# Layer 1's causal attention: 32 steps of one query block each, or 16 steps of blocks i and 7-i together

## The chip, the cores and the metric

The kernel runs on one core of a Trainium2 chip. A core has a matrix engine (TensorE, PE in the profile, with its weight loads as PEld), a vector engine (VectorE, DVE), an activation engine (ScalarE, ACT), a general engine (GpSimd, POOL) and SyncE (SP), which issues most transfers. Each works through its own instructions in order, and they wait for each other by semaphores. SBUF is the working memory of 128 partitions; PSUM takes TensorE's results, in 8 banks of 512 float32 numbers for each partition. The metric is the device time of one execution in microseconds (us), as the median of several runs.

## The reference, cut to what matters

Two transformer layers on x of shape (2, 1024, 256). Each layer adds an attention and a feed-forward of the same normalized input. The change concerns the attention of the second layer, which has 16 heads, queries of 128 + 64 numbers and keys and values that all heads share (64 numbers of latent and 64 rotated ones):

```python
q = rmsnorm(hidden_states @ wq_a.T, q_a_ln_w) @ wq_b.T          # 16 heads x (128 + 64)
ckv = hidden_states @ wkv_a.T                                    # 64 + 64, one for all heads
kv = rmsnorm(ckv[..., :64], kv_a_ln_w)
q_pe, k_pe = apply_rope(q_pe, cos, sin), apply_rope(k_pe, cos, sin)
q_abs = jnp.einsum('bhsd,hdc->bhsc', q_nope, q_absorb)
scores = (einsum('bhsc,btc->bhst', q_abs, kv) + einsum('bhsd,bxtd->bhst', q_pe, k_pe)) * SCALE
attn = softmax(where(causal, scores, finfo.min))                 # 1024 x 1024, lower triangle
x = jnp.einsum('bhst,btc->bhsc', attn, kv)
x = jnp.einsum('bhsc,hdc->bhsd', x, out_absorb)                  # then @ wo.T
```

A query block is 128 tokens, and there are 8 for each of the 2 batches. Block i needs keys 0 to 128(i+1) only, so block 0 has 128 keys and block 7 has 1024.

## The kernel before, in words

The first 764 us compute layer 0, the feed-forward of layer 1 and the projections that its attention needs; weights are folded there, so that a query of two heads comes out of three small matmuls (`wpe`, `folded["wm"]`, `folded["w2"]`) and the output needs one product with `folded["wvo"]`. The keys lie in `kT`, the values four times over the partitions in `vrep`. The attention follows as one order written out by hand (`tc.manual_schedule()`): each engine runs its instructions in the order in which the code names them, while the loads on SP are placed by the scheduler where they fit.

A step is a batch b, a query block i and a half g of the 16 heads, so 32 steps. Batch 0 goes from block 0 up to block 7, batch 1 from block 7 down to block 0. At any time three steps overlap: `s` computes scores, `prev` (the step before) is multiplied with the values, and `older` (two before) is normalized and projected to the output.

- `scores(s, h)`: TensorE multiplies a head's query with the keys into a PSUM pair (2 banks, L1055). VectorE adds the mask, writes the result to `p` and reduces the row's maximum, all in one instruction (L1060). ScalarE takes the exponential and its sum (L1063). A block with more than 512 keys takes a whole pair for a head; with 512 or fewer, two heads share a pair, one bank each.
- `turn_over` (L1068): VectorE transposes the weights in 32 x 32 squares into `pT`.
- `product(s, sb)` (L1094): eight small matmuls side by side in the array for each block of 32 values, into `ps_o`, which takes 4 banks.
- `inverse`, `inverse_T`, `normalize`: 1/sum is spread by GpSimd (L1075), transposed by TensorE (L1083), copied by ScalarE (L1087), and multiplied with `ps_o` by VectorE (L1103).
- `output` and `add` (L1115, L1125): the projection, and the addition to the row of x that was fetched from memory.
- `query_half`: the query of a coming step: `project` (L988, L994) on TensorE into a pair, `latent` (L1027) on ScalarE, `rotate` (L1009 to L1020) on VectorE, ScalarE and GpSimd. `t1` and `t2` are single buffers.

PSUM holds two pairs under the tag "s", which scores, queries, transposes and outputs take in turn, and the one `ps_o`: all 8 banks. For blocks 4 to 7 a step has four cycles of two heads, for blocks 0 to 3 two cycles of four heads. Each cycle first names its scores, then in cycle 0 the normalization and the next query, in cycle 1 the output, in the last the transposes, then a share of the products, then the turn-overs. A step has 4(i+1) value blocks, dealt over one to four cycles by a rule of its size.

## The time and the profile before

| | us |
|---|---|
| median of 3 runs (1473.28 to 1475.24) | 1473.69 |
| the profiled execution's own time | 1469.04 |
| its span, first to last instruction | 1467.3 |
| TensorE busy | 1327.6 |
| VectorE busy | 790.8 |
| ScalarE busy | 671.2 |
| GpSimd busy | 443.8 |
| first score of layer 1's attention | 770.00 |

The span is what the profile's lines add up to; the run's own time has a little more around it. A row of the profile names the line of the code, the engine, the operation, the tile written and those read, the shape, the count, the busy time and the mean of one, and the idle time ahead of it with what ended that. TensorE's times are modelled at their ends, so a busy TensorE need not be at its peak; the granted clock says how much of its full speed it had.

### The profile page before, as it was taken

Reading aid. Unit: us, or ns where it says so; the run is one execution under the profiler, and the core shown is the slowest. Engines: PE = TensorE matmul, PEld = TensorE weight load, DVE = VectorE, ACT = ScalarE, POOL = GpSimd, SP = SyncE. Lnnn points to the kernel's source line nnn. Section 1 sums busy time; section 2 is a strip of 40 time slices with the busy share of each in tenths; the row PEclk is TensorE's granted clock in tenths of the full one; section 3 lists DMA queues with packets and bytes.
Section 4 is the critical chain, followed back from the end, with each engine's and each line's share of the span. In section 5 each row is a group of like instructions: output and inputs, shape, how many; then the busy total and the mean of one; then the engine's idle time right before and its main releaser. Section 6 shows DMA issues by size and latency. Waiting matters only on the chain.

```text
span 1467.3 us, 36387 instructions
## 1 busy us (share of the span) xinstructions
PE 1327.6 (90%) x15614; PEld 795.9 (54%) x15614; DVE 790.8 (54%) x1939; ACT 671.2 (46%) x1234; POOL 443.8 (30%) x480
## 2 busy tenths in 40 slices
PE   5689999898999989999996777999999999998886
PEld 2233445354563533465775554666666676665565
DVE  3765545454456553134333455666777767665543
ACT  2234563453638546643314444545454454444442
POOL 2223433333414211003304332434233233423330
PEclk9659999899999999999996999999999999999988
DMA  5121301010100000001233000000000000000000
GB/s 202 55 34 57 99 8 23 0 23 1 23 5 18 23 1 18 15 1 54 73 88 49 12 10 4 13 13 13 13 3 14 13 3 14 13 14 13 9 9 16
DMA packets 56977, 39.27 MB, mean 27 GB/s; under 512 B 37200, under 2 KB 52816, under 8 KB 56560
## 3 DMA queue, kind: packets, MB, share of 16 engines
q1 hardware_dynamic: 55968, 33.67, 8.5%
q8 instruction: 122, 2.00, 0.6%
q0 software_dynamic: 416, 2.49, 0.4%
q10 hardware_dynamic: 432, 0.79, 0.2%
q14 instruction: 39, 0.32, 0.1%
HBM read 24.35 MB, written 10.49 MB: 24 GB/s over the span
## 4 chain that ended last, share of the span: by engine, by line
PE 85%; DVE 7%; ACT 3%; issue 2%; POOL 2%; DMA 1%; SPq 0%; DVEq 0%; ACTq 0%; POOLq 0%
PE ps_s L1055 19%; PE ps_m L307 11%; PE ps_o L1094 10%; PE ps_m L558 6%; PE ps_t L1115 5%; PE ps_o L373 5%; PE ps_m L461 4%; PE ps_m L430 4%; PE ps_t L988 4%; PE ps_m L228 3%; PE ps_m L573 3%; PE ps_t L994 2%; DVE p L1060 2%; PE ps_s L307 1%; PE ps_t L1083 1%
## 5 line engine op out<-in xcount | busy, mean ns | idle before, releaser
L1055 PE MATMUL ps_s<-kT,qc 128*128 128x512 f32 (+3 forms) x768 | 304.1, 525 | 70.8 <-DVE nmax L1060 67.1
L1063 ACT ACTIVATE p<-p,nmax 128x128 f32<-128x128 f32 (+7 forms) x256 | 198.3, 775 | 289.9 <-DVE nmax L1060 289.0
L1060 DVE CUSTOM_DVE_ANT_0 p<-ps_s,maskw 128x128 f32<-128x128 f32 (+7 forms) x256 | 193.6, 757 | 219.3 <-PE ps_s L1055 218.2
L1055 PEld LDWEIGHTS ps_s<-kT,qc 128*128 128x128 f32 x768 | 133.9, 198 | 205.4 <-DVE nmax L1060 104.5
L355 ACT ACTIVATE p<-ps_s 128x1024 f32<-128x1024 f32 (+1 forms) x192 | 152.8, 809 | 165.0 <-PE ps_s L348 159.9
L307 PE MATMUL ps_m<-head,head 16*128 16x512 f32 (+3 forms) x672 | 192.5, 547 | 20.8 <-DVE nmx L318 14.0
L1068 DVE STREAM_TRANSPOSE pT<-p 128x128 f32<-128x128 f32 (+7 forms) x256 | 185.9, 755 | 7.9 <-ACT p L1063 7.9
L348 PE MATMUL ps_s<-head,head 17*128 17x512 f32 (+3 forms) x768 | 170.8, 550 | 0.0
L1020 POOL TENSOR_TENSOR qc<-t,t 32x512 f32<-32x512 f32 x124 | 158.6, 1279 | 15.8 <-DVE t L1016 8.0
L1094 PE MATMUL ps_o<-pT,vrep 32*64 32x128 f32 x9216 | 153.1, 275 | 3.9 <-issue 3.9
L1094 PEld LDWEIGHTS ps_o<-pT,vrep 32*64 32x64 f32 x9216 | 134.8, 131 | 22.9 <-issue 21.0
L307 PEld LDWEIGHTS ps_m<-head,head 16*128 16x128 f32 x672 | 71.4, 187 | 120.1 <-DVE nmx L318 37.1
L358 POOL TENSOR_SCALAR_AFFINE_SELECT p<-p 128x256 f32<-128x256 f32 x128 | 51.4, 408 | 240.1 <-ACT p L355 238.9
L1075 POOL COPY rb<-rinv 128x512 f32<-128x512 f32 x32 | 19.6, 612 | 342.2 <-DVE rinv L1073 342.1
L323 DVE TENSOR_REDUCE nmx<-ps_m 128x1 f32<-128x512 f32 x112 | 72.2, 686 | 44.0 <-PE ps_s L348 35.3
L558 PE MATMUL ps_m<-xnT,w 128*128 128x512 f32 x192 | 94.4, 620 | 0.0
L318 DVE CUSTOM_DVE_ANT_0 junk<-ps_m,maskz,nmx 128x512 f32<-128x512 f32 (+3 forms) x112 | 57.7, 548 | 59.6 <-PE ps_s L348 45.1
L373 PE MATMUL ps_o<-p,v 128*32 128x512 f32 (+3 forms) x768 | 82.5, 502 | 0.0
L1115 PE MATMUL ps_t<-wvo,xT 128*128 128x256 f32 x256 | 72.7, 436 | 1.7 <-DVE xT L1103 1.7
L461 PEld LDWEIGHTS ps_m<-wpr,hT 128*128 128x128 f32 x512 | 61.2, 196 | 17.1 <-issue 6.6
L318 DVE CUSTOM_DVE_ANT_0 junk<-ps_m,maskz 128x512 f32<-128x512 f32 (+3 forms) x112 | 50.5, 487 | 34.3 <-PE ps_s L348 31.6
L461 PE MATMUL ps_m<-wpr,hT 128*128 128x128 f32 x512 | 67.3, 286 | 0.0
(174 smaller groups left out, 1770.3 us busy)
## 6 DMA issues: line engine op xcount, KB each, us to landing
rows<-proj SPq DMA_DIRECT2D x12, 512.0 KB, 2.6
stage<-rows SPq DMA_DIRECT2D x96, 64.0 KB, 3.1
w<-in_w SPq DMA_DIRECT2D x3, 768.0 KB, 4.6
x_sb<-in_x SPq DMA_DIRECT2D x4, 512.0 KB, 12.2
x<-x_sb SPq DMA_DIRECT2D x4, 512.0 KB, 3.1
fold_wo<-in_wo SPq DMA_DIRECT2D x8, 256.0 KB, 3.4
xin<-x SPq DMA_DIRECT2D x16, 128.0 KB, 2.2
vrep<-kv SPq DMA_DIRECT2D x32, 64.0 KB, 2.1
```

The costliest lines, as they stand in the source:

```text
L307: nc.tensor.matmul(t[:, :w], quad(q, c, D0)[:, i * P : (i + 1) * P], quad(k, c, D0)[:, k0 : k0 + w], start=True, stop=True, tile_position= ...
L348: nc.tensor.matmul(t[:, c % 2, :w], quad(k, c, D0 + 1)[:, j * P : (j + 1) * P], quad(q, c, D0 + 1)[:, at : at + w], start=True, stop=True, ...
L355: nc.scalar.activation(p[:, pair[0] : pair[0] + 2, :w], t[:, :, :w], AF.Exp)
L373: nc.tensor.matmul(quad(box["o"], c)[:, SC - w :], values[g][:, j, 32 * c : 32 * c + 32], p[:, c, :w], start=(j == 0), stop=(j == 4 * iq + ...
L461: nc.tensor.matmul(po[:, :P], f["h", hc // 2][:, hc % 2, t * P : (t + 1) * P], wpr[:, hc, cols], start=(hc == 0), stop=(hc == NH0 - 1),)
L558: nc.tensor.matmul(pw, w1t[f"w{i + 1}"][:, kc, hc * P : (hc + 1) * P], xnT1[n // 2][:, kc, (n % 2) * SC : (n % 2 + 1) * SC], start=(kc == ...
L1020: (one, two)[x].tensor_tensor(qc[b, i][64 + 32 * x : 96 + 32 * x, g, hh], t1[at : at + 32], t2[at : at + 32], ALU.add,)
L1055: nc.tensor.matmul(sc[:, n0:n1], qc[s.b, s.i][:, s.g, h // QP, h % QP, :], kT[:, s.b * S + n0 : s.b * S + n1], start=True, stop=True,)
L1060: nc.vector.tensor_tensor_reduce(p[:, :w], sc, maskw[:, S - w :], -1.0, 3.0e38, ALU.add, ALU.min, nmax)
L1063: nc.scalar.activation(p[:, :w], p[:, :w], AF.Exp, bias=nmax, scale=-1.0, accum_out=s.rsum[:, h : h + 1])
L1068: nc.vector.transpose(s.pT[:, : s.nsb, h, :], s.p[h][:, : 32 * s.nsb])
L1094: nc.tensor.matmul(s.o[64 * hh : 64 * hh + 64, c, : QP * 32], vrep[32 * c : 32 * c + 32, s.b * 32 + sb, :], s.pT[32 * c : 32 * c + 32, sb, ...
```

## The change

A step now is a batch, a half of the heads and two blocks: i (7, 6, 5 or 4) and 7-i (0, 1, 2 or 3), which together always have 9 x 128 keys. There are 16 steps, in the order 7, 6, 5, 4 for each batch, with both halves g of each. Every step has four equal cycles. A cycle names the scores of two heads of the wide block (`k` = 0), each with a pair of PSUM, then of two heads of the narrow one (`k` = 1), which share a pair, then nine of the 36 value blocks of the step before, and then one dense item: a query of the next step (cycles 0 and 2), the output of both blocks (cycle 1) or the transposes (cycle 3). The turn-overs of the four heads follow.

Tiles hold both blocks: `rsum`, `rinv`, `rb`, `rT`, `xT`, `xin` have a dimension of 2 more, `ps_o` uses 256 of 512 columns in each bank, `pT` has 36 blocks. `p` has three buffers in place of four, since two narrow heads share one, `rb`, `rT`, `xT` and `xin` one in place of two or three. Queries are kept for one step, with four buffers `qc`; each loads its own cosines and sines unless it is in the first two steps, whose angles lie with the mask in the unused part of the tile `wpe` and are loaded behind it. In `project` the matmuls of `w2` come first. `rotate` always copies to `t1` by ScalarE, copies `t2` from `t1`, and multiplies on GpSimd (on VectorE ahead of the first step).

```diff
-        trig = main.tile([P, 2, P], F32, tag="trig", name="trig")
...
-                        for k_, key in enumerate(("cosq", "sinq")):
-                            nc.sync.dma_start(trig[:, k_], a[key][:, :P])
...
                     wpe = main.tile([P, 8 * E], F32, tag="wC", name="wpe")
+
+                    maskw = wpe[:, NPAIR * P + 4 * P :]
+                    trig = wpe[:, NPAIR * P : NPAIR * P + 4 * P].rearrange("p (k t) -> p k t", k=4)
...
+                    for k_, i in enumerate((TB - 1, 0)):
+                        for x_, key in enumerate(("cosq", "sinq")):
+                            nc.sync.dma_start(
+                                trig[:, 2 * k_ + x_], a[key][:, i * P : (i + 1) * P]
+                            )
...
+            def rotate(self, ahead=False):
...
+                t1 = att.tile([P, QP, P], F32, tag="t1", name="t1")
+                nc.scalar.copy(t1.rearrange("p r t -> p (r t)"), self.pe)
+                self.latent()
+                t2 = att.tile([P, QP, P], F32, tag="t2", name="t2")
                 for lo, hi in ((0, 64), (64, 0)):
+                    nc.scalar.copy(t2[lo : lo + 64], t1[hi : hi + 64])
+                one.tensor_tensor(t1, t1, cos, ALU.mult)
                 one.tensor_tensor(t2, t2, sin, ALU.mult)
...
+        def scores(s, k, h):
+
+            w = P * (s.blocks[k] + 1)
+            lo = 0
+            if k == 0 or h % 2 == 0:
                 s.sc = pair("s").rearrange("p k c -> p (k c)")
+                s.pp = att.tile([P, S], F32, tag="p", name="p", bufs=3)
+            else:
+                lo = SC
+            sc, p = s.sc[:, lo : lo + w], s.pp[:, lo : lo + w]
...
+                    sc[:, n0:n1], s.q[k].qc[:, h // QP, h % QP, :],
                     kT[:, s.b * S + n0 : s.b * S + n1], start=True, stop=True,
...
         with tc.manual_schedule():
+            steps = [(b, i, g) for b in range(B) for i in range(TB - 1, TB // 2 - 1, -1) for g in range(2)]
...
+            for q in ahead(steps[0]):
+                q.project()
+                q.rotate(ahead=True)
...
             for at in range(len(steps) + 2):
                 s = new_step(*steps[at]) if at < len(steps) else None
+                nxt = ahead(steps[at + 1]) if at + 1 < len(steps) else ()
+                cycles = NCY if s is not None else 1
+                for c in range(cycles):
+                    heads = [] if s is None else [(k, 2 * c + h) for k in range(2) for h in range(2)]
+                    if c == 0 and older is not None:
+                        normalize(older, 0)
+                        fetch_x(older)
+                    if c == 2 and older is not None:
+                        add(older)
+                    for k, h in heads[:1]:
+                        scores(s, k, h)
+                    if c == 0 and older is not None:
+                        normalize(older, 1)
+                    for k, h in heads[1:]:
+                        scores(s, k, h)
+                    if prev is not None:
+                        for sb in range(c * NSB // cycles, (c + 1) * NSB // cycles):
+                            product(prev, sb)
+                    q = nxt[c // 2] if nxt and c % 2 == 0 else None
+                    if q is not None:
+                        q.project()
+                    if c == min(1, cycles - 1) and older is not None:
+                        output(older)
+                    if prev is not None:
+                        if c == 0:
+                            inverse(prev)
+                        if c == cycles - 1:
+                            inverse_T(prev)
+                    for k, h in heads:
+                        turn_over(s, k, h)
+                    if q is not None:
+                        q.rotate()
+                if s is None and older is not None:
+                    add(older)
                 older, prev = prev, s
```

## The prediction

> **What bounds the kernel now.** I read the busy shares first, then the windows cut at each step's first score matmul, then who TensorE waited for, and last the timeline of a wide and of a narrow step. The page:

> ```profile
> PE 1327.6 (90%) x15614; PEld 795.9 (54%) x15614; DVE 790.8 (54%) x1939; ACT 671.2 (46%) x1234; POOL 443.8 (30%) x480
> L1055 PE MATMUL ps_s<-kT,qc 128*128 128x512 f32 (+3 forms) x768 | 304.1, 525 | 70.8 <-DVE nmax L1060 67.1
> L1060 DVE CUSTOM_DVE_ANT_0 p<-ps_s,maskw 128x128 f32<-128x128 f32 (+7 forms) x256 | 193.6, 757 | 219.3 <-PE ps_s L1055 218.2
> ```

> TensorE is the fullest engine, and its idle time in this stage stands before the scores, waiting for the reduction of L1060. Layer 1's attention runs from the first score at 770.00 to the end at 1467.3: 697.3 us. Windows of four of its 32 steps (blocks 7, 4, 3 and 1; columns: window, length, busy PE, PEld, DVE, ACT, POOL, clock, DMA):

> ```profile
> 1116.42:1144.09 27.67, 27.67 (x594) 18.09 (x589) 20.24 (x28) 13.33 (x23) 8.20 (x7) 1.00 0.01 3
> 1269.92:1291.90 21.98, 21.05 (x466) 15.38 (x461) 14.51 (x28) 10.91 (x23) 8.19 (x7) 1.00 0.01 3
> 1334.01:1354.60 20.59, 17.42 (x321) 11.19 (x317) 12.08 (x28) 9.43 (x21) 6.93 (x6) 1.00 0.04 10
> 1413.85:1431.27 17.42, 13.92 (x193) 10.47 (x189) 7.84 (x28) 7.50 (x21) 6.95 (x6) 0.90 0.05 12
> ```

> Wide steps are TensorE's alone: no idle time. Narrow ones (blocks 0 to 3) idle 3.2 to 3.5 us of 17 to 21. The waits and the timelines, block 7 and then block 3, say why:

> ```profile
> PE ps_s L1055 <- DVE nmax L1060: 67.1, 73, 6.6
> 1118.45 1.22 DVE L1060 CUSTOM_DVE_ANT_0 p<-ps_s,maskw 128x1024 f32<-128x1024 f32 x1 [0.53 <-PE ps_s L1055]
> 1119.73 1.09 PEld L988 LDWEIGHTS ps_t<-qnT,wpe 128*128 128x128 f32 x8 [0.43 <-DVE nmax L1060]
> 1120.16 1.22 DVE L1060 CUSTOM_DVE_ANT_0 p<-ps_s,maskw 128x1024 f32<-128x1024 f32 x1 [0.48 <-PE ps_s L1055]
> 1335.17 0.69 DVE L1060 CUSTOM_DVE_ANT_0 p<-ps_s,maskw 128x512 f32<-128x512 f32 x1 [2.26 <-PE ps_s L1055]
> 1335.93 0.30 PEld L1055 LDWEIGHTS ps_s<-kT,qc 128*128 128x128 f32 x2 [1.62 <-DVE nmax L1060]
> 1337.09 0.69 DVE L1060 CUSTOM_DVE_ANT_0 p<-ps_s,maskw 128x512 f32<-128x512 f32 x1 [1.22 <-PE ps_s L1055]
> 1338.70 0.30 PEld L1055 LDWEIGHTS ps_s<-kT,qc 128*128 128x128 f32 x2 [1.62 <-DVE nmax L1060]
> ```

> The last four lines carry the forecast. Two narrow heads share one PSUM pair, each in its own half; the second head's weights load at 1335.93, just after the reduction of the first (1335.17 + 0.69) has ended, and again at 1338.70. The second half of a pair is not written while the first is unread. The changed kernel keeps "two narrow heads in one pair", and its built order has that same wait on the second narrow head of every cycle.

> [...] products follow scores and are followed by them within the 2.02 us of their 128 matmuls (1122.93 to 1124.95)[...].

> **The change, part by part.** The same matmuls, reductions, exponentials and transposes run, but in 16 steps of 4 cycles. TensorE's cycle: two wide heads (w0, w1), two narrow (n0, n1), 9 value blocks, one dense item.

> Measured pieces, from the start of the first score: the reduction of w0 starts at 2.03 / 1.81 / 1.59 / 1.38 us and that of w1 at 3.74 / 3.31 / 2.88 / 2.46 for blocks 7 / 6 / 5 / 4 (block 7: lines above minus 1116.42). The next VectorE instruction starts 1.15 / 1.02 / 0.89 / 0.75 after a wide reduction does. From the start of a narrow reduction to the load that waits for it: 0.35 / 0.48 / 0.62 / 0.76 for 128 to 512 keys. From a 512-wide load to its reduction 1.16 (1335.93 to 1337.09), to TensorE's next item 0.96; narrower ones by 0.21 less for each 128 keys. 9 value blocks: 144/128 of 2.02 = 2.28.

> VectorE takes w0, w1, n0, n1 in order, so n1 loads only after w1 *and* n0 are reduced. Blocks 7 and 0: 3.74 + 1.15 + 0.35 = 5.24; with n1 (0.40) and the products the dense item starts at 7.92. Without the wait it would be w1's end 3.44 + 0.63 + 2.28 = 6.35. For 6/1, 5/2, 4/3 the same sum gives 7.64, 7.42 and 7.43 (for 4/3 n0's own matmul ends last: 2.27 + 1.16 + 0.76 = 4.19, then 0.96 + 2.28), against about 6.27 without. The new wait costs 1.1 to 1.6 us in each of 64 cycles, some 83 us. Queued behind n1 on TensorE are the products and the dense item.

> Dense items of one step: two projections at 3.05 (1119.96 to 1122.93 for one), 16 output matmuls 3.65 (eight took 1.89), eight transposes 1.2 (four took 0.60): 10.9. After a projection w1 needs the pair that ScalarE empties with three copies at 0.59: ready 1.95 after the projection, while w1 could start at 1.71 / 1.50 / 1.29 / 1.08; that costs 0.24 to 0.87, twice a step. A normalization between w0 and w1 in cycle 0 pushes w1 by 0.05 to 0.24. Steps: 4 x 7.92 + 10.9 + 0.5 = 43.1; 42.5; 42.1; 42.6. Four of each: 681.

> Corrections: step 0 has no products, outputs or transposes and is held by VectorE, 30.4 instead of 43.1; that leaves VectorE 1.2 late into step 1, which lacks the output (-3.7); step 15 projects nothing (-7.8). Sum 681 - 12.7 + 1.2 - 3.7 - 7.8 = 658.

> Before step 0: t1 is a single buffer, so the second query's copy waits for the first's additions. Project 762.15 to 765.3; three copies and two of t2 to 768.4; two products and two additions 1.4 + 2.7 to 772.5, GpSimd's to 773.1; then the second query: 2.9 + 1.4 + 2.7, so the first reduction starts near 780.3 (776.74 now), as if scores began at 778.3. I add 2.5 for half clock in step 0 (0.66 in the first window now). After step 15: copies and normalization 2.2, 36 value blocks 9.1, output 3.6, transposes 1.2, copies and normalization 1.7, output 3.6, addition and store 3.8: 25. Total 778.3 + 2.5 + 658 + 25 = 1464 against the span of 1467.3: 3 us less, 0.2%. No row shows a narrow reduction behind a wide one, so the wait is bounded by 1.0 below (n0's reduction never later than its own matmul) and 1.6 above (every hand-over between engines 0.3 longer); I take 1.3, and each end moves the total by 19 us. The two edges may be off by 5.

> At nothing: cosine and sine loads of the first pair now queue on SP behind `wpe` near 747, four at about 0.5 us; their first use is at 768, and 32 `vrep` loads behind them (till 786.8) are first needed past 800. The other steps issue 4 loads each, 56 in place of 30, and each waits for the rotation two steps back; SP has nothing else in 42 us. The projection's two narrow matmul groups now come before the wide ones, the same work. t1 goes through ScalarE and GpSimd always, and t2 is copied from it: 16 x 0.59 and about 16 x 1.27 us more, on engines under 50% full. GpSimd needs 7.8 us per query, two in 42 us, and the next step needs only the first half of the second query, 8.4 us after its projection; slack about 4. VectorE's cycle ends near 8.6 us of 9 to 12. If that cover went, n0 would wait the difference once a step.

> **Rivals.** (1) *The wait is harmless and TensorE is full*: 64 x 1.3 = 83 us less, near 1388 us; for it speaks that wide steps now idle 0.0; against it the block 3 lines. Half of it, were n0's reduction to slip ahead of w1's, 1430. (2) *Slower by the clock*: idle gaps in each cycle could drop TensorE to half speed. At one 5 us window a step, 2.5 us lost, it is 16 x 2.5 = 40 us: 1511. It decides from about 0.2 us a step, since the sum above has only 3 to give. Against it: block 3's 15% idle time kept 1.00, and the new cycle idles 1.1 to 2.5 of 11. (3) *The wait is at its upper end*, 19 us more: 1490; the block 7 step, which has few hand-overs, can't exclude it. That the change doesn't do what it says can't be: the built order has the 16 steps, with 72 product matmuls in each cycle.

> **The numbers.** Profiled run 1469.04, median 1473.69; 3 us less gives 1470.5. The forecast has 0.65 (own range 1455 to 1487; 0.33 faster, 0.13 within, 0.19 slower), rival 1 with its half 0.12, rival 2 0.10, rival 3 0.13. Faster 0.45, same 0.13 (0.2% is about what a measurement of this kernel can tell), slower 0.42. The range 1428 to 1508 reaches to the half of rival 1 and nearly to rival 2, and leaves out some 0.15.

> **What would show it.** PEld waiting for L1064 (the new reduction line) once per cycle, 64 times at 1.5 us or more; steps of 42 to 43 us; 1.00 clock from step 2 on; VectorE near 60% and never the last in steps 2 to 14. I am wrong if steps take 36 us (no wait), or if the clock column shows less than 0.95 in the middle, or if w1 waits for ScalarE longer than 0.9 us.

## The result: no measurable change

The changed kernel takes 1470.39 us (median of 12 runs, 1468.56 to 1478.67), the kernel before 1471.57 us beside it; the ratio is 1.0008, with a 95% interval of 0.9986 to 1.0030. The forecast was 1470.5, 0.2% less. The profiled execution took 1475.92 us with a span of 1474.2, so the traces are compared by stage and not by their ends. Of the four executions of the first combined version below, one was slow (1644.12 us, at a mean clock of 0.73), and its figures are those of the other three.

The page of the changed kernel, first busy time of each engine, then its two rows of the score matmul (busy, mean ns of one, idle time ahead and what ended it):

```profile
PE 1317.6 (89%) x15614; PEld 781.1 (53%) x15614; DVE 770.3 (52%) x1893; ACT 671.6 (46%) x1250; POOL 460.4 (31%) x494
...
L1059 PE MATMUL ps_s<-kT,qc 128*128 128x512 f32 (+3 forms) x768 | 290.7, 506 | 84.3 <-DVE nmax L1064 68.1
...
L1059 PEld LDWEIGHTS ps_s<-kT,qc 128*128 128x128 f32 x768 | 129.8, 191 | 221.7 <-DVE nmax L1064 98.2
```

The row of the matmul waits 68.1 us for the reduction, where it waited 67.1 before. The wait is as large as it was; it has only moved to other places. The waits of the attention (total, number, longest) give the count:

```profile
PEld ps_s L1059 <- DVE nmax L1064: 98.2, 71, 1.6
...
PE ps_s L1059 <- DVE nmax L1064: 68.1, 67, 2.6
...
PE ps_s L1059 <- ACT qc L1008: 12.0, 24, 0.9
```

On TensorE that is one wait for each of 64 cycles and three more in steps 0 and 1. Before, 16 narrow steps had four each, also 64. The windows show what changed around them. First the kernel before, in its first eight steps (blocks 0 to 3), the sixteen wide ones, the last eight, and as a whole (length, busy PE, PEld, DVE, ACT, POOL, clock, DMA share, GB/s):

```profile
770.00:923.27 153.27, 115.44 (x1485) 81.14 (x1485) 73.46 (x224) 67.21 (x172) 59.85 (x50) 0.87 0.10 19
923.27:1312.54 389.27, 379.73 (x7812) 261.85 (x7809) 273.14 (x432) 192.55 (x352) 131.03 (x112) 1.00 0.04 11
1312.54:1467.34 154.80, 123.96 (x2040) 88.10 (x2036) 72.09 (x227) 60.16 (x161) 43.45 (x39) 0.90 0.04 11
770.00:1467.34 697.34, 619.12 (x11328) 431.08 (x11328) 418.68 (x883) 319.92 (x685) 234.33 (x201) 0.95 0.05 13
```

And the changed kernel, from step 1 to step 14, and as a whole:

```profile
817.88:1409.21 591.33, 519.33 (x9954) 358.02 (x9953) 345.63 (x731) 281.85 (x620) 232.31 (x200) 1.00 0.05 14
779.29:1474.22 694.93, 600.07 (x11328) 411.85 (x11328) 398.01 (x837) 319.93 (x700) 251.00 (x215) 0.98 0.06 16
```

From first score to end TensorE's busy time fell by 19.0 us and its idle time rose by 16.7 (78.2 to 94.9). The fall is mostly clock: the narrow steps had run at 0.87 and 0.90, which is about 71 us at half speed (2 x 0.13 x 153 + 2 x 0.10 x 155), and the changed kernel has about 21 of those, all in step 0 and after the last scores. Inside these stretches TensorE was busy for 60.3 us before and for 16.4 now; half of the difference, 22 us, is my estimate of what the clock gave, from the kernel before, where eight output matmuls took 3.62 us at a clock of 0.50 (1406.38) and 1.89 at 1.00 (1350.32). It is enough for the whole fall. So the pairing kept TensorE at full clock in the narrow blocks and gave nearly the same time back in idle stretches. With 1.6 us more ahead of the first score, the attention from its first projection on took 704.4 us (769.80 to 1474.22), and 705.2 before.

A block 7 cycle of the changed kernel (timeline; start, length, what, idle time before it):

```profile
1155.35 3.82 PE L1059 MATMUL ps_s<-kT,qc 128*128 128x512 f32 x10
...
1159.03 1.21 DVE L1064 CUSTOM_DVE_ANT_0 p<-ps_s,wpe 128x1024 f32<-128x1024 f32 x1
...
1160.16 0.28 DVE L1064 CUSTOM_DVE_ANT_0 p<-ps_s,wpe 128x128 f32<-128x128 f32 x1
...
1160.51 0.30 PEld L1059 LDWEIGHTS ps_s<-kT,qc 128*128 128x128 f32 x2 [1.53 <-DVE nmax L1064]
1160.51 0.49 PE L1059 MATMUL ps_s<-kT,qc 128*128 128x128 f32 x2 [1.34 <-DVE nmax L1064]
1160.93 2.08 PEld L1107 LDWEIGHTS ps_o<-pT,vrep 32*64 32x64 f32 x144
...
1163.18 0.97 PEld L994 LDWEIGHTS ps_t<-qnT,wm 64*128 64x128 f32 x16 [0.17 <-issue]
```

The ten matmuls are w0, w1 and n0 (w for the two wide heads, n for the two narrow ones, as in the prediction). The reductions of w1 (1159.03) and n0 (1160.16) follow each other on VectorE, and only then n1's weights load, 5.16 us after the cycle began (forecast 5.24). The dense item begins at 7.83 (forecast 7.92).

### The profile page after: what moved, and what is told of

Same layout as the page of the kernel before. It is cut to its first block, busy times and chain, and to the rows that moved or that the text cites. A ratio compares the mean times of both kernels' runs of the same rounds, so it can differ in the third digit from the quotient of the medians.

```text
span 1474.2 us, 36254 instructions
## 1 busy us (share of the span) xinstructions
PE 1317.6 (89%) x15614; PEld 781.1 (53%) x15614; DVE 770.3 (52%) x1893; ACT 671.6 (46%) x1250; POOL 460.4 (31%) x494
## 4 chain that ended last, share of the span: by engine, by line
PE 77%; DVE 11%; ACT 5%; issue 4%; POOL 2%; DMA 1%; SPq 0%; ACTq 0%; DVEq 0%; POOLq 0%
PE ps_s L1059 12%; PE ps_m L307 11%; PE ps_o L1107 10%; DVE p L1064 6%; PE ps_m L558 5%; PE ps_o L373 5%; PE ps_m L461 4%; PE ps_m L430 4%; PE ps_t L1001 4%; PE ps_t L1130 4%; PE ps_m L228 4%; PE ps_t L994 2%; PE ps_m L573 2%; ACT qc L1008 2%; ACT t L1018 1%
## 5 line engine op out<-in xcount | busy, mean ns | idle before, releaser
L1059 PE MATMUL ps_s<-kT,qc 128*128 128x512 f32 (+3 forms) x768 | 290.7, 506 | 84.3 <-DVE nmax L1064 68.1
L1064 DVE CUSTOM_DVE_ANT_0 p<-ps_s,wpe 128x128 f32<-128x128 f32 (+7 forms) x256 | 189.7, 756 | 217.2 <-PE ps_s L1059 216.7
L1059 PEld LDWEIGHTS ps_s<-kT,qc 128*128 128x128 f32 x768 | 129.8, 191 | 221.7 <-DVE nmax L1064 98.2
L1073 DVE STREAM_TRANSPOSE pT<-p 128x128 f32<-128x128 f32 (+7 forms) x256 | 175.3, 742 | 0.0
L1107 PEld LDWEIGHTS ps_o<-pT,vrep 32*64 32x64 f32 x9216 | 135.5, 131 | 37.4 <-issue 35.9
L1023 POOL TENSOR_TENSOR t<-t,cosq 128x512 f32<-128x512 f32 x28 | 35.7, 1274 | 293.9 <-issue 203.3
L1018 ACT COPY t<-ps_t 128x512 f32<-128x512 f32 x32 | 18.8, 586 | 146.5 <-PE ps_t L1001 126.0
L430 PE MATMUL ps_m<-xnT,wfc 128*128 128x512 f32 x128 | 68.6, 661 | 0.2
```

Source lines behind the costliest of these rows:

```text
L1059: nc.tensor.matmul(sc[:, n0:n1], s.q[k].qc[:, h // QP, h % QP, :], kT[:, s.b * S + n0 : s.b * S + n1], start=True, stop=True,)
L1064: nc.vector.tensor_tensor_reduce(p, sc, maskw[:, S - w :], -1.0, 3.0e38, ALU.add, ALU.min, nmax)
L1073: nc.vector.transpose(s.pT[:, at, h, :], s.p[k, h])
L1107: nc.tensor.matmul(s.o[64 * hh : 64 * hh + 64, c, k * P : (k + 1) * P], vrep[32 * c : 32 * c + 32, s.b * 32 + sb, :], s.pT[32 * c : 32 * c ...
```

## The experiments

**Both narrow matmuls first.** The theory says that the wait of n1 costs 1.1 to 1.6 us in each cycle. The matmul and the reduction were parted, so that n0's and n1's matmuls stand ahead of both reductions; n1 then writes its half while n0's is still unread, and no wait is needed.

```diff
...
-                    for k, h in heads[1:]:
+                    for k, h in heads[1:2]:
                         scores(s, k, h)
+                    narrow = [(k, h, multiply(s, k, h)) for k, h in heads[2:]]
+                    for args in narrow:
+                        reduce(s, *args)
...
```

> The changed kernel, with both narrow matmuls of a cycle named ahead of both narrow reductions, so that the second half of the pair is written before VectorE has read the first. Theory (the second narrow head waits for VectorE's queue and that costs 1.1 to 1.6 us in each of 64 cycles): the wait for the narrow reduction goes from the waits of TensorE, the dense item of a cycle starts near 6.3 us instead of 7.4 to 7.9, steps take 36.5 to 37.5 us instead of 42 to 43, and the time falls by 75 to 90 us, to 1380 to 1395. Rival (the wait is harmless, something else, such as ScalarE's hand-back of the query's pair or VectorE's own queue, sets the pace of a cycle): steps stay above 40 us and the time above 1440. A change between the two would mean that a second limit lies just behind the wait.

Measured: 1396.39 us, ratio 0.9504 (0.9465 to 0.9542) to the kernel before. Against the changed kernel's 1.0008 that is 5.0%, 74 us, or 1.16 for each of 64 cycles. The score row of its page, and the window of steps 1 to 14:

```profile
L1059 PE MATMUL ps_s<-kT,qc 128*128 128x512 f32 (+3 forms) x768 | 274.6, 498 | 22.1 <-ACT qc L1008 11.8
```

```profile
806.18:1331.16 524.98, 505.74 (x9953) 361.11 (x9953) 341.00 (x732) 280.25 (x620) 231.68 (x199) 1.00 0.06 16
```

The reduction is gone as the first cause of waiting, and the 14 steps take 66.4 us less. Only 52.8 of that was idle time (72.0 to 19.2); the other 13.6 is busy TensorE. Cycle 3, which ends in the short transposes, shows the price by pair, from its first score to the next: 9.08 to 7.50 us for blocks 7/0, 9.08 to 7.70 for 6/1, 9.08 to 7.92 for 5/2, 9.19 to 8.14 for 4/3.

**The same edit in the kernel before.** This separates what the pairing is worth from what the wait costs.

```diff
...
-                    for h in heads:
-                        scores(s, h)
+                    together = 1 if s is None or s.i >= 4 else 2
+                    for h0 in range(0, len(heads), together):
+                        some = [(h, multiply(s, h)) for h in heads[h0 : h0 + together]]
+                        for h, sc in some:
+                            reduce(s, h, sc)
```

> The kernel before with the same edit alone: in blocks 0 to 3 both matmuls of a shared pair are named ahead of the two reductions; steps, cycles and queries stay as they were. Theory: the idle 3.2 to 3.5 us of each of 16 narrow steps is this wait, so 40 to 55 us go, to 1417 to 1432; what is left to the pairing of blocks is then some 30 us. Rival (narrow steps are held by VectorE, 12 of 20.6 us busy, or by ScalarE): less than 15 us go.

Measured: 1405.55 us, ratio 0.9562 (0.9526 to 0.9599), 64 us less, more than the 40 to 55 expected. Windows of the same three stretches as above:

```profile
776.66:900.04 123.38, 103.95 (x1484) 79.03 (x1484) 71.13 (x224) 63.73 (x172) 59.77 (x50) 0.90 0.13 24
900.04:1289.80 389.76, 380.02 (x7813) 261.89 (x7808) 273.15 (x432) 192.55 (x352) 131.30 (x113) 1.00 0.04 12
1289.80:1406.74 116.94, 104.28 (x2040) 80.13 (x2036) 69.05 (x227) 56.66 (x161) 43.61 (x39) 1.00 0.05 15
```

The wide steps took the same 389 us; both narrow stretches lost 30 and 38. In each, idle *and* busy TensorE fell (busy by 11.5 and 19.7), in the last one with the clock going from 0.90 to 1.00. What I had missed is that the wait cost twice: its own length, and the half clock that came with it (71.7 us of it from the first score on, 23.9 without the wait).

Together: without the wait the attention from its first projection takes 637.9 us in the old order (768.81 to 1406.74) and 629.4 in the new one (762.00 to 1391.4). So the pairing itself is worth some 9 us, with intervals of the two ratios that overlap; most of the gain lay in the wait, which both kernels have 64 times. What the later versions add to it, some 20 us, came from the order behind it and from the start.

**Value blocks between the narrow heads.** Here n1 still waits for n0's reduction, but nine value blocks stand in front of it.

```diff
-                    for k, h in heads[1:]:
+                    for k, h in heads[1:3]:
                         scores(s, k, h)
                     if prev is not None:
                         ...
                             product(prev, sb)
+                    for k, h in heads[3:]:
+                        scores(s, k, h)
```

> The changed kernel, with the nine value blocks of a cycle moved between the first and the second narrow head. The second matmul still waits for the first's reduction as the program orders it, but 2.3 us of other work stand in front of it. Theory: the wait is a matter of what TensorE has to do meanwhile, so it shrinks below 0.3 us a cycle and the time falls as in the run with both matmuls first, to 1380 to 1400. Rival (not the wait, but VectorE's or ScalarE's pace holds the cycle): within 20 us of the changed kernel, 1450 to 1475.

Measured: 1441.75 us, ratio 0.9811 (0.9775 to 0.9846), 29 us less than the changed kernel: outside both ranges. A step of block 4 (the last of batch 0) shows which half was right, in us from first score to first score:

| | cycle 0 | 1 | 2 | 3 |
|---|---|---|---|---|
| changed kernel | 10.61 | 11.82 | 10.43 | 9.19 |
| products between | 11.30 | 10.77 | 9.57 | 8.36 |
| both first | 9.55 | 10.76 | 9.37 | 8.14 |

In cycles 1 to 3 covering the wait works as well as removing it, to within 0.2 us. In cycle 0 it does not. Cycle 3 now ends with n1's reduction and the turn-overs right behind it, so VectorE is still turning over when the next step begins, and the normalization and the reduction of w0 come late. The timeline of this step's cycle 0, whose first score is at 1048.85:

```profile
1048.62 2.75 DVE L1073 STREAM_TRANSPOSE pT<-p 128x640 f32<-128x640 f32 x4
...
1051.29 0.65 DVE L1117 TENSOR_TENSOR xT<-ps_o,rT 128x512 f32<-128x512 f32 x1
...
1051.87 0.81 DVE L1064 CUSTOM_DVE_ANT_0 p<-ps_s,wpe 128x640 f32<-128x640 f32 x1
...
1052.84 1.10 PE L1059 MATMUL ps_s<-kT,qc 128*128 128x512 f32 x2 [0.79 <-DVE nmax L1064]
```

The reduction of w0 starts 3.02 us after the first score, where it was 1.42 in the changed kernel, and n0, which takes over the pair of w0, waits for it: 14 times in cycle 0 of steps 1 to 14, 11.3 us in all, and never in cycles 1 to 3. These steps take 29 us more than with both matmuls first; the time after them takes 11.5 more and the start some 4, which I did not follow further.

TensorE's busy time over steps 1 to 14 was also 11.5 us above the run with both first (517.25 to 505.74), 0.2 for each cycle, in which TensorE goes one more time from full matmuls to value blocks and back. The prediction reckoned with the 2.02 us of the 128 products in its row, and had no term for such a change.

**A longer wait.** A copy on VectorE ahead of each first narrow reduction lengthens what n1 waits for; nothing reads its result. First 128x512, then 128x1024.

```diff
+            if k == 1 and h % 2 == 0:
+                nc.vector.tensor_copy(filler, kT[:, :SC])
```

> The changed kernel with one more VectorE instruction, a copy of 128x512 float32 between two SBUF tiles that nothing reads, just ahead of each cycle's first narrow reduction (64 of them). Theory: the narrow wait is on the path and set by VectorE's queue, so each copy of d us adds d to the wait in its cycle: with d between 0.4 and 0.7 the time rises by 25 to 45 us, to 1495 to 1515; blocks 4 and 3 rise by 0.2 less a cycle, since there the matmul itself ends last. Rival (VectorE's queue has slack here): below 8 us more.

> The changed kernel with the filler copy twice as long, 128x1024 float32 ahead of each first narrow reduction. The copy of 128x512 took 0.42 us and cost 42 us in all. Theory A (the wait is on the path and VectorE's queue delays the next cycle as well): twice that, 80 to 90 us more than the changed kernel, 1550 to 1560, clock 1.00 nearly throughout. Theory B (in the run with the short filler the clock fell to 0.85 to 0.89 in four windows that hold an idle gap of about 2.3 us ahead of the second narrow head; with gaps of 2.7 it falls in nearly every cycle of blocks 7 and 6): another 30 to 70 us on top, 1585 to 1625, with a clock below 0.95 in those steps.

Measured: 1512.45 us (ratio 1.0286, 1.0239 to 1.0332) and 1543.82 us (1.0497, 1.0457 to 1.0537), 41 and 72 us above the changed kernel. The first lies in theory's range; the second in neither: the long copy took less than twice the short one, and the clock, which theory A wanted at 1.00 and theory B made cost 30 to 70 us, cost less than B said. The same step of block 5, first of the changed kernel, then with the short copy, then with the long one, each line from its own kernel:

```profile
985.18:1026.86 41.68, 37.15 (x714) 25.79 (x713) 24.57 (x53) 20.28 (x44) 16.34 (x15) 1.00 0.07 21
```

```profile
999.48:1042.49 43.01, 37.14 (x714) 25.77 (x713) 25.90 (x57) 20.28 (x44) 16.75 (x15) 1.00 0.07 20
```

```profile
1008.10:1052.19 44.09, 37.15 (x714) 25.77 (x713) 26.98 (x57) 20.72 (x44) 17.25 (x15) 1.00 0.07 20
```

The copies took 0.42 and 0.69 us there, and the steps are 1.33 and 2.41 us longer: four times the copy less 0.09 (1.32 and 2.40). So in this step every further tenth on VectorE lands on TensorE's path, and VectorE had 0.1 us of slack in a cycle, not more. The total is a sum of three: 40.0 us of copies in the first run and 57.1 in the second (the rows of the copy: 64 of 625 and 893 ns), less 64 x 0.09 = 6, and a remainder of about 7 and 21 us. That is the clock: with the same matmuls, TensorE's busy time in steps 1 to 14 rose from 519.3 to 526.3 and 541.8 us, by 7.0 and 22.5, and the attention has 34.4 and 73.1 us at half clock in place of 21.1. What stood ahead of the falls of the clock is in the last section, as are copies of more than 0.42 us, which lift the mean.

**What stands behind the wait.** With both matmuls first, most steps took 37 to 38 us with some 36.3 of busy TensorE. More than half of the rest is w1 waiting for ScalarE's copies (11.1 of the 19.2 idle us of steps 1 to 14), and three places for the dense item and the products tell whether it can be hidden: three value blocks ahead of the dense item and six behind it, or all nine behind it, and then the same with two buffers for `t1` and `t2`.

```diff
+                    for sb in mine[:cut]:
+                        product(prev, sb)
                     q = nxt[c // 2] if nxt and c % 2 == 0 else None
                     ...
+                    for sb in mine[cut:]:
+                        product(prev, sb)
```

> Both narrow matmuls first, as in the first run, and of the nine value blocks of a cycle three now stand ahead of the dense item and six behind it. Theory: what is left in a step of 37 to 38 us above its 36.3 us of busy TensorE is w1 waiting for ScalarE's (or VectorE's) emptying of the pair that the dense item filled; 1.5 us of products between hide it, so up to 1 us a step goes, 10 to 15 us. Against it: the run with the products between the narrow heads showed about 0.23 us more busy TensorE for each further change between value blocks and other matmuls, 64 x 0.23 = 15 us. So 1380 to 1400, even with the first run. Rival (VectorE holds the steps): no change and no more busy TensorE.

> Both narrow matmuls first, then the dense item, then all nine value blocks: 2.3 us of products behind the dense item, with no further change of kind. Theory as for the split: w1 no longer waits for ScalarE (it would be ready 1.95 us after a projection), and the dense item waits up to 0.5 us for the reduction of w1 in blocks 7 and 6, none in 5 and 4. Steps 36 to 36.8 us, the time 1375 to 1388; after the last step the output stands ahead of the last products and saves about 2 us more. Rival: VectorE's queue, 24.3 of 37 us, is next, and the time stays within 5 us of the first run's 1396.

> As the run before it, with two buffers each for t1 and t2, so that the second query ahead of step 0 is copied while the first is rotated. Theory: the first reduction, 17.9 us after the first projection in the changed kernel, comes 3 to 4 us earlier, and the time falls by 2 to 4 us; nothing changes in the later steps. Rival (the first reduction is held by VectorE's and GpSimd's rotation alone): under 1 us.

In the first of these `cut` is 3, in the other two 0, and there the last output also stands ahead of the last products.

Measured: 1391.34 (0.9462, 0.9418 to 0.9507), 1397.38 (0.9484, 0.9436 to 0.9532) and 1389.87 us (0.9448, 0.9411 to 0.9486). The first two are not told apart from the 0.9504 of both matmuls first by the medians, but the windows are plain: a step of block 7 and one of block 4 with the split, then with the dense item first.

```profile
1064.53:1101.86 37.33, 37.27 (x717) 26.21 (x712) 24.30 (x52) 19.41 (x44) 16.32 (x15) 1.00 0.04 10
989.17:1026.85 37.68, 37.68 (x717) 25.92 (x713) 24.19 (x53) 20.28 (x44) 16.40 (x15) 1.00 0.04 10
```

```profile
1108.93:1150.46 41.53, 36.77 (x717) 26.05 (x713) 24.22 (x52) 19.84 (x44) 16.79 (x15) 1.00 0.07 22
996.18:1032.52 36.34, 36.34 (x717) 25.79 (x713) 24.07 (x53) 19.94 (x44) 16.39 (x15) 1.00 0.04 10
```

The split leaves TensorE next to no idle time, but has 1.0 to 1.4 us more of busy TensorE a step than both matmuls first alone (36.2 and 36.3). With the dense item first there is neither in block 4; in block 7 the dense item waits for w1's reduction, 0.9 to 1.0 us of TensorE each, and 4.8 us of this step are idle, 3.7 of them in these waits and 1.1 in a break that the profile puts down to "issue". My estimate of "up to 0.5 us" was too small, and the time lies outside theory's range and within the rival's: in blocks 7 and 6 VectorE's reduction is indeed next. Two buffers for `t1` and `t2` bring the first reduction from 17.9 to 14.7 us after the first projection, and step 1 begins 5.2 us earlier (39.1 in place of 44.2), more than the 2 to 4 expected.

**All of it together**, the split for blocks 7 and 6 and the dense item first for 5 and 4:

```diff
...
+                    cut = 3 if s is not None and s.blocks[0] >= 6 else 0
...
```

> The three parts that helped, together: both narrow matmuls first; for blocks 7 and 6 three value blocks ahead of the dense item and six behind it, for blocks 5 and 4 all nine behind it; two buffers each for t1 and t2. Theory: steps 37.1 to 37.4 us for blocks 7 and 6 (as in the run that split everywhere), 36.0 to 36.4 for 5 and 4 (as in the run with the dense item first), the start 3 to 5 us shorter: 1391 - 8 x 1.3 - 4 = 1376, range 1370 to 1385. Rival (the gains share one slack, so that they do not add): 1388 or more.

> As the combined version, with two value blocks instead of three ahead of the dense item for block 6. Theory: with none ahead the dense item waited 0.3 to 0.9 us a cycle for w1's reduction there, with three it waited 0.0; two blocks are 0.5 us, so the steps of block 6 stay within 0.2 us of 37.1 and the time within 3 us of the combined version, 1378 to 1385; steps of blocks 5 and 4 at 36.0 to 36.8, of block 7 at 37.3, the first reduction 14.7 us after the first projection. Rival (the switch between kinds of matmul is what costs, not the wait): the same again, since both versions switch as often; a difference of more than 3 us would speak against both.

Measured: 1382.01 us (0.9400, 0.9366 to 0.9434), and with two value blocks instead of three for block 6, 1378.58 us (0.9361, 0.9322 to 0.9401); both in the ranges expected, so the gains of the parts add. Their intervals overlap, so these two do not tell the cost of a wait from that of a change of kind. The second has these steps of blocks 7, 6, 5 and 4, and steps 1 to 14 in its last line:

```profile
1057.33:1094.66 37.33, 37.27 (x716) 26.20 (x712) 24.69 (x53) 19.75 (x45) 16.03 (x15) 1.00 0.04 10
1131.99:1168.84 36.85, 36.85 (x718) 26.37 (x713) 24.23 (x54) 20.13 (x45) 16.35 (x15) 1.00 0.04 11
1241.70:1278.05 36.35, 36.19 (x716) 26.24 (x712) 24.34 (x53) 20.03 (x44) 16.33 (x15) 1.00 0.08 24
984.58:1020.92 36.34, 36.34 (x716) 25.78 (x712) 24.06 (x53) 19.94 (x44) 16.39 (x15) 1.00 0.03 10
803.68:1315.37 511.69, 509.41 (x9952) 363.56 (x9952) 339.71 (x733) 281.32 (x622) 232.82 (x201) 1.00 0.06 16
```

TensorE idles 2.3 of 511.7 us. It is now what rival 1 had supposed of the changed kernel, 6.4% faster than both kernels.

## Why the prediction was right

**The new wait**, the main term: right in place, number and size. Without it cycle 3 became shorter by 1.58, 1.38, 1.16 and 1.05 us; the forecast's own differences are 1.57, 1.37, 1.15 and 1.16. Over all 64 cycles the removal gave 74 us where 83 were reckoned. In steps 1 to 14 these differences ask for 72 us, and 66.4 were measured. w1's wait for ScalarE is no reason, since it is 11.1 us in both kernels. But in the run with both matmuls first some cycles are 0.7 to 1 us longer than their like, with breaks that the profile puts down to "issue", most of them at the value blocks: 7.0 us of TensorE, where the changed kernel has 2.5. Their cause stays open. The second head's wait was seen in each of the 64 cycles, at 1.4 to 1.6 us of the weight loader but for three cycles of steps 0 and 1 (0.8 to 1.0), so "1.5 us or more" holds roughly; TensorE itself stood idle for only 0.8 to 1.3 of it (0.5 once), and the rest of the price is busy time. I take it that two heads in one run of matmuls pay one end where they paid two; no run measures that alone.

**Steps.** Forecast 43.1, 42.5, 42.1 and 42.6 us for blocks 7, 6, 5 and 4; measured means from step 2 on 43.2, 42.4, 41.9 and 42.4. Step 1 took 40.4 (40.6). From the first projection to step 1 it was 48.1 us (49.05). w1's wait for ScalarE was 0.3, 0.5 and 0.7 us of TensorE for blocks 6, 5 and 4, where 0.45, 0.66 and 0.87 were forecast.

**The end** is the term that failed: 59.8 us from step 15's first score on, measured 65.0. "36 value blocks 9.1" took 14.4 (timeline):

```profile
1446.02 7.43 PE L1107 MATMUL ps_o<-pT,vrep 32*64 32x128 f32 x360 [2.09 <-DVE xT L1117]
...
1455.12 2.10 PE L1107 MATMUL ps_o<-pT,vrep 32*64 32x128 f32 x128 [1.67 <-issue]
...
1458.87 1.58 PE L1107 MATMUL ps_o<-pT,vrep 32*64 32x128 f32 x88 [1.66 <-issue]
```

They begin after 2.1 idle us, and the clock is 0.57 in their first 4; two breaks of 1.67 come on top, again only "issue". These 5.2 us, less 2.6 by which the rest was reckoned too long, turn a forecast of 701.9 from the first projection into 704.4, and a gain of 3 us into one of 0.8; the measurement can tell neither from nothing. That the two medians, forecast and measured, lie within 0.2 us of each other is luck: the forecast started from 1473.69 for the kernel before, which took 1471.57 beside the changed one, its terms missed by 5.2 and 2.6 us, and its own range was 1455 to 1487.

**Ahead of the attention** the profiled execution was 7.7 us later than that of before (769.80 to 762.15), in the part of the program that the change leaves alone but for four loads. In the other traces the same part ended between 762.0 and 770.2, so one execution cannot carry a difference of a few us.

**At nothing**: the added loads, ScalarE's and GpSimd's added work cost TensorE next to nothing, as forecast. TensorE's weight loader waited for GpSimd's `qc` once after step 0, for 0.5 us. VectorE was at 58% in steps 1 to 14, but "never the last" was too confident: it had 0.1 us a cycle.

**Rivals.** Rival 1 (harmless wait) fell by the run with both matmuls first. Rival 3 (upper end) fell by the steps. Rival 2, the clock, did not happen (1.00 in steps 1 to 14), but it was nearer than I thought, as the last section shows, and I had the sign of the clock the wrong way round: the kernel before was the one that lost by it, 71 us at half speed. My sum contained this unseen, because I took the new steps from pieces measured at full clock and compared them with the whole old stage.

## What to carry to other kernels

A shared buffer with two writers and one reader makes the order of the program into a wait: name both writes ahead of both reads, or put other work between them, before the work is re-tiled. Removing that wait was worth 64 us in the kernel before and 74 in the changed one; the re-tiling without it 9. When two versions come out equal, compare busy time, idle time and clock by stage: here -19 and +17 us hid behind a zero.

## What the runs showed of the hardware that I had not expected

```profile
1400.89:1404.31 3.42, 1.50 (x6) 0.62 (x5) 1.46 (x5) 2.56 (x5) 0.34 (x1) 1.00 0.00 0
1404.31:1407.72 3.41, 2.88 (x8) 1.92 (x7) 1.53 (x6) 1.86 (x8) 3.27 (x3) 0.50 0.00 0
1407.72:1411.13 3.41, 3.41 (x26) 2.53 (x32) 1.11 (x4) 0.28 (x2) 2.69 (x3) 0.50 0.00 0
```

```profile
1156.57:1159.98 3.41, 1.01 (x5) 0.57 (x4) 2.53 (x5) 2.55 (x5) 3.33 (x3) 1.00 0.07 19
1159.98:1163.39 3.41, 3.41 (x114) 3.19 (x121) 2.92 (x6) 0.78 (x4) 3.22 (x4) 0.50 0.09 24
...
1282.86:1286.27 3.41, 1.67 (x6) 0.76 (x4) 2.45 (x5) 2.81 (x6) 2.51 (x3) 1.00 0.04 10
1286.27:1289.69 3.42, 2.57 (x140) 2.23 (x145) 2.63 (x7) 1.34 (x6) 3.29 (x3) 1.00 0.12 33
```

In the first line TensorE is busy for 44%, and most of its idle time is one wait for the reduction, of 1.77 us at 1403.08; the half clock follows. In the second run a stretch with 1.01 us of busy TensorE (30%) is followed by half clock, one with 1.67 (49%) is not, though the gap in the second case is the longer one (2.59 us to 2.41): it lies across the border of two stretches. Counted over the attention in the traces of the two kernels, from the stretch of the first score on, all 8 stretches at full clock with TensorE busy for less than 44% were followed by half clock, 7 of 12 between 44 and 55%, and none of 361 above. The way back took more: all 13 stretches at half clock below 88% were followed by another, none of the 14 above 94% was, and none lay between. This fits the narrow steps of the kernel before, idle for 15 to 20%, which kept the half clock once they had it, as the second line shows (84% busy). The changed kernel's emptiest stretch in steps 1 to 14 was busy for 57%. These shares hold for this stage: ahead of it, in the same two traces, 7 stretches at full clock that the profile calls 57 to 100% busy were also followed by half clock.

**Some copies on VectorE lasted until GpSimd was done.** The short copy took 0.42 us in some cycles and 0.96 or 1.3 in others. A cycle of block 7:

```profile
1217.10 1.27 POOL L1025 TENSOR_TENSOR t<-t,sinq 128x512 f32<-128x512 f32 x1
...
1217.69 0.96 DVE L1066 COPY filler<-kT 128x512 f32<-128x512 f32 x1
...
1218.91 0.49 PE L1060 MATMUL ps_s<-kT,qc 128*128 128x128 f32 x2 [2.19 <-DVE nmax L1067]
```

GpSimd's instruction ends at 1218.37, the copy 0.28 later. Two cycles of block 6 show the same: the copies that begin at 924.76 and 1238.30 took 1.25 and 1.26 us, and each ended 0.28 us after the GpSimd instruction that ran when it began (from 924.46 and 1238.01, 1.27 us each). The copy at 1226.84, with GpSimd idle from 1223.78 to 1229.15, took 0.42. What holds the copy back is not shown. The reductions, which read PSUM, kept their lengths: in steps 1 to 14 of the changed kernel those of 128x1024 took at most 1.23 us, beside a busy GpSimd (1170.44) and alone (1180.08).
